# A dilated convolution by points on one core: matmuls issued in halves of the output rows, constants loaded on another queue, a second input's first points made later

## The chip, the cores and the metric

The kernel runs on one core of a Trainium2 chip. The metric is the device time of one execution in microseconds; less is better. PE is the matrix engine, DVE, ACT and POOL the vector, scalar and GpSimd engines, SP the engine that only issues transfers.

## What is computed

Input x is 4 images of 256 channels, 64x64, in float32. The part that the change touches is the first convolution and the weights that it uses:

```python
k = conv(x, w1, padding=6, rhs_dilation=2) + b1      # 256 -> 128 channels, 7x7
k = conv(k, w2) + b2                                 # 128 -> 49, 1x1
attn = softmax(k, axis=1)                            # 49 logits at every pixel
xp = pad(x, 6)
shifts = stack([xp[:, :, 2*u:2*u+64, 2*v:2*v+64] for u in range(7) for v in range(7)])
y = sum over the 49 taps of shifts * attn            # local attention
...
h = relu(bn(conv1x1(y, 256 -> 64)))
h = relu(bn(conv3x3(h, 64 -> 64)))
return relu(bn(conv1x1(h, 64 -> 256)) + y)
```

Batch norm uses the batch's own statistics. Everything from the softmax on lies after the changed stages.

## The kernel before

**The convolution by points.** w1 and w2 are composed into one 7x7 weight from 256 channels to 49 logits. Along the rows the convolution is evaluated at points: four pairs +p, -p and a last pass with the points 0 and infinity, so five passes n = 0 to 4. A pass needs its points (tile xi, x0 and x1 by strip), made on DVE from the row-sorted input (tile slots), and its weights, `weights(n, half)`. The 256 input channels are taken as two halves of 128 (`half` 0 and 1): all five passes are run for the first, then all five for the second.

**Strips.** The picture's columns are cut into four strips of eight. `column_convs(s, u, first)` (L247) does strip s, for x0 and x1 (i) and each of its eight columns (w): matmuls (L261) whose stationary operand is 128 columns of xi, and whose moving operand is 49 to 343 columns of weights. They add up in eight PSUM banks, acc[i][d], d = s-1, s, s+1. Two strips, half a picture, are 50 calls; a float32 matmul is two records in the profile, so 100 records.

**The first channel half.** Its passes after the first go in two half-pictures h, two strips each (loop at L466). `visit` makes the points of two strips (first `apply_factor` on the slots where the pass needs it; then `even`, `odd` and `mix`), `column_convs` uses them, and `put_aside` (L285, L286) copies finished banks to sv (three buffers) and stores them on ACT's queue in DRAM. DVE's and PE's order in this part is the order of the code (a manual schedule). Before it, `product` (L318) makes the weights of both channel halves by matmuls (L330) with w1 stationary, strided as loaded (w1raw) or copied (w1v); DVE and ACT write them out (L341 to L347).

**The second channel half is prepared meanwhile.** `fill_stage(h)` (L443) loads a half-picture of its 128 channels in 16 transfers on SP (L450, three raw buffers) and sorts them with 64 ACT copies (L169) into one tile, stage. `stage_parts(h)` (L453) makes pass 0's unmixed points x0 and x1 of the two strips, 12 DVE operations, and stores them (L459, SP); `stage_rows` (L462) stores the sorted rows, 4864 KB. Since there is one stage tile, `fill_stage(1)` comes behind `stage_parts(0)`. `load_ready` (L437) and `finish_parts` (two DVE operations per strip) bring the points back and mix them; `load_rows` (L430) brings the sorted rows into slots.

**The second channel half.** For each strip `put_back` (L612) loads what was put aside (L618 on SP, bks has four buffers), copies it on ACT into the PSUM banks (L619), and `column_convs` adds to it. `outputs` (L590; ACT copy L602, DVE L603, L604 and four more) turns two finished strips into logits. SP's order is by hand in pass 0; the rest is a scheduler's.

**Small loads.** Between the two channel halves, 16 small loads are issued on ACT's queue (L505 to L515): an identity, 1x1 weights, averaging and mask matrices, and batch norm parameters, in part of one element per partition. All are used behind the convolution.

`HALVES` is `(slice(0, 64), slice(64, 128))`. The local attention (L767), the 1x1 convolution (L800) and the moments (L1047) issue their matmuls in such halves already.

Of the kernel before, what the change touches and what calls it, by code (L numbers as in the profile page):

```python
# [48 lines left out]
P = 128  # L49
B, C, H, W = 4, 256, 64, 64  # L50
NH = C // P
K7 = 7
K = K7 * K7
PAD = 6
NT = H // 8
MID = 64
EPS = 1e-5
Q = 4
R = W // 2
# [9 lines left out]
NS, WS = 4, 8  # L69
# [7 lines left out]
CW = 16  # L77
# [17 lines left out]
def conv_seq_kernel(ctx: ExitStack, tc: tile.TileContext, xp, xt, w1, b1, w2t, b2, m1t, g1, be1,  # L95
# [154 lines left out]
    def column_convs(s, u, first):  # L250

        for d in (s - 1, s, s + 1):
            if not 0 <= d < NS:
                continue
            for i in range(2):
                for w in range(WS * s, WS * s + WS):
                    lo, hi = strip_taps(d, w)
                    if lo >= hi:
                        continue
                    o = (w - 3 + lo - WS * d) * K  # L260
                    nc.tensor.matmul(  # L261
                        acc[i][d][:, o : o + (hi - lo) * K],
                        xi[:, i, CW * w : CW * w + CW, :].rearrange("p x t -> p (x t)"),
                        u[i][:, lo * K : hi * K],
                        start=(first and w == max(0, WS * d - 3)),
                        stop=(w == min(R - 1, WS * d + WS + 2)),
                        skip_group_check=True,
                    )

    bks = pool(ctx, "bkp", 1).tile([P, 4, WS * K], F32, name="bks")  # L270
    n_back = [0]
# [2 lines left out]
    with ExitStack() as s1:  # L274
# [13 lines left out]
        with ExitStack() as s2:  # L288
# [29 lines left out]
            def product(w1raw, half, v, pw):  # L318

                wv = w1raw[:, :, v::K7].rearrange("p c u -> p u c")  # L320
                if half:
                    t = rawp.tile([P, 24, WP], F32, tag="raw", name="w1v").rearrange("p r w -> p (r w)")
                    t = t[:, : K7 * P].rearrange("p (u c) -> p u c", c=P)
                    nc.scalar.copy(t, wv)
                    wv = t
                for u in range(K7):

                    o = 0 if u == 0 else (2 + NP) * K if u % 2 else K
                    n = (1 + NP) * K if u in (0, K7 - 1) else NP * K
                    nc.tensor.matmul(  # L330
                        pw[:, o : o + n],
                        wv[:, u, :],
                        powers[:, u, :n],
                        start=(u == 0),
                        stop=(u == K7 - 1),
                        skip_group_check=True,
                    )
                c = slice((6 - v) * K, (7 - v) * K)
                ue = ut[:, half, 1 : 1 + NP, c]
                uo = pw[:, (2 + NP) * K : (2 + 2 * NP) * K].rearrange("p (i k) -> p i k", k=K)  # L340
                nc.scalar.copy(ue, pw[:, K : (1 + NP) * K].rearrange("p (i k) -> p i k", k=K))  # L341
                nc.scalar.copy(
                    ut[:, half, :: 1 + 2 * NP, c],
                    pw[:, : 2 * (1 + NP) * K].rearrange("p (a k) -> p a k", a=2)[:, :, :K],
                )
                nc.vector.tensor_tensor(ut[:, half, 1 + NP : 1 + 2 * NP, c], ue, uo, ALU.subtract)
                nc.vector.tensor_tensor(ue, ue, uo, ALU.add)  # L347
# [105 lines left out]
        def stage_parts(h, strips=range(2)):  # L453
            for s in strips:
                row = rows_of(stage, strip(s))
                for i, part in enumerate((even, odd)):
                    x = stgp.tile([P, SW, NT], F32, tag="x%d" % i, name="stage_x")
                    part(PAIRS[0], squares, row, x)
                    nc.sync.dma_start(out=ready[:, 2 * h + s, i], in_=x)  # L459
# [6 lines left out]
        for n, (p, factor, left) in enumerate(passes):  # L466
            if n == 0:
                continue
            u = weights(n, 0)
            for h in range(2):  # L470
                if factor is not None and (n, h) != (1, 0):
                    apply_factor(slots, factor, NR - 1 if n == 1 else NR - 2, strip(2 * h, 2))
                visit(slots, strip(2 * h, 2), p, left)
                if (n, h) == (2, 1):
                    stage_parts(0)
                    fill_stage(1)
                if (n, h) == (4, 0):
                    stage_parts(1, [0])
                    for s in range(2):
                        load_rows(s)  # L480
                if (n, h) == (4, 1):
                    stage_parts(1, [1])
                    load_ready(0)
                    finish_parts(0)
                    apply_factor(stage, squares[0], NR - 1)
                    stage_rows(1)
                    load_ready(1)
                    finish_parts(1)
                    for s in range(2):
                        apply_factor(slots, squares[0], NR - 1, strip(s))  # L490
                for s in range(2 * h, 2 * h + 2):
                    column_convs(s, u, True)
                    put_aside(n, s)
# [8 lines left out]
    pdiff_sb = late.tile([P, P], F32, name="pdiff_sb")  # L502
    bn12 = late.tile([P, 4], F32, name="bn12")
    bn3 = late.tile([P, 2, NH], F32, name="bn3")
    nc.scalar.dma_start(out=ident, in_=z)  # L505
    nc.scalar.dma_start(out=w1m, in_=m1t)
    nc.scalar.dma_start(out=pavg_sb, in_=pavg)
    nc.scalar.dma_start(out=pdiff_sb, in_=mask)
    for g in range(2):
        half = slice(g * MID, (g + 1) * MID)  # L510
        nc.scalar.dma_start(out=w3m[half, :], in_=m3t)
        for i, a in enumerate((g1, be1, g2, be2)):
            nc.scalar.dma_start(out=bn12[half, i : i + 1], in_=a[:, None])
    nc.scalar.dma_start(out=bn3[:, 0, :], in_=g3.rearrange("(n p) -> p n", p=P))
    nc.scalar.dma_start(out=bn3[:, 1, :], in_=be3.rearrange("(n p) -> p n", p=P))  # L515

    smp = pool(ctx, "smp", 2)
    outer = pool(ctx, "outerp", 1).tile([P, OUTER], F32, name="outer")

# [73 lines left out]
    def outputs(n, p, g):  # L593

        d = 2.0 * p * p
        for q in PAIRS:
            if q != p:
                d *= p * p - q * q
        m, t = (combs[:, 2 * i + n_combs[0] % 2] for i in range(2))
        n_combs[0] += 1  # L600
        a0, a1 = (accall[:, 4 * g + i : 4 * g + i + 3 : 2, : WS * K] for i in range(2))
        nc.scalar.copy(m, a0)  # L602
        nc.vector.tensor_tensor(t, a1, m, ALU.add)  # L603
        nc.vector.tensor_tensor(m, m, a1, ALU.subtract)  # L604
        for j in range(4):
            src, dst = (v.rearrange("p s v -> p (s v)") for v in (m if j % 2 else t, logit[:, g, j]))
            if n == 0:
                dst, src = (v.rearrange("p (w k) -> p w k", k=K) for v in (dst, src))
                stt(dst, src, p**j / d, bias_s)
            else:  # L610
                stt(dst, src, p**j / d, dst)
# [10 lines left out]
    with tc.manual_schedule(engines={mybir.EngineType.SP}):  # L622
        for s in range(2):
            put_back(0, s)
        for s in range(NS):
            if s in (1, 2):
                load_ready(s + 1)
                put_back(0, s + 1)
                load_rows(s + 1)
            if s > 1:  # L630
                finish_parts(s)
            column_convs(s, weights(0, 1), False)
            if s > 1:
                outputs(0, PAIRS[0], s - 2)
    for n, (p, factor, left) in enumerate(passes):
        if n == 0:
            continue
        u = weights(n, 1)
        if p is None:
            for s in range(NS):  # L640
                visit(slots, strip(s), p, left)
            for t in pads:
                nc.gpsimd.memset(t, 0.0)
        for s in range(NS):
            if n == 2 and s == NS - 1:
                apply_factor(slots, factor, NR - 2, strip(s))
            if p is not None:
                visit(slots, strip(s), p, left)
            if n == 1 and s:
                apply_factor(slots, passes[2][1], NR - 2, strip(s - 1))  # L650
            for d in ([s] if s == 0 else []) + ([s + 1] if s + 1 < NS else []):
                put_back(n, d)
            column_convs(s, u, False)
            if p is None:
                for d in range(s - 1 if s else 0, s + 1 if s == NS - 1 else s):
                    last_outputs(d)
            elif s > 1:
                outputs(n, p, s - 2)
            if p is None and 0 < s < NS - 1:
                if s == 2:  # L660
                    turn(0, 0)
                exponents(s - 1)
                shares(s - 1)
# [487 lines left out]
```

## Time and profile before

| | |
|---|---|
| median of three runs | 783.74 us (782.07 to 786.91) |
| the profiled execution | 784.71 us |
| its span | 782.9 us, 13023 instructions |
| mean granted clock of PE | 0.974 of full |
| matmuls of the convolution, L261 | 2000 records |
| points on DVE, L150 on the arena | 192 operations, 293.4 us |

The profile is of one execution. A group's line has the source line, engine, operation, what is written and read, the shape and the count; then busy time and the mean ns of one; then the engine's idle time ahead of them with what ended most of it. In the timeline, a line is a run of like operations: start, length, and in brackets the idle time before it and its releaser.

Where the 100 records of each half-picture of conv begin in the trace: 48.25 (pass 0, strips 0 and 1), 89.10, 107.84 (pass 1), 127.77, 149.92 (pass 2), 168.63, 188.20 (pass 3), 206.99, 225.71 (pass 4), 244.44; then the second channel half, passes 0 to 4, from 263.16, 308.29, 348.24, 387.48 and 424.94. The last ends near 466 us. All that follows, to 782.9, comes behind it.

### The profile page before, as it was taken

Reading aid. Unit: us, or ns where it says so; the run is one execution under the profiler, and the core shown is the slowest. Engines: PE = TensorE matmul, PEld = TensorE weight load, DVE = VectorE, ACT = ScalarE, POOL = GpSimd, SP = SyncE. Lnnn points to the kernel's source line nnn. Section 1 sums busy time; section 2 is a strip of 40 time slices with the busy share of each in tenths; the row PEclk is TensorE's granted clock in tenths of the full one; section 3 lists DMA queues with packets and bytes.
Section 4 is the critical chain, followed back from the end, with each engine's and each line's share of the span. In section 5 each row is a group of like instructions: output and inputs, shape, how many; then the busy total and the mean of one; then the engine's idle time right before and its main releaser. Section 6 shows DMA issues by size and latency. Waiting matters only on the chain.

```text
span 782.9 us, 13023 instructions
## 1 busy us (share of the span) xinstructions
PE 716.9 (92%) x5232; PEld 579.5 (74%) x5232; DVE 578.8 (74%) x685; ACT 304.7 (39%) x601; POOL 90.0 (12%) x155
## 2 busy tenths in 40 slices
PE   1969898999999979989999999999989988987995
PEld 1959787888888868868888888987878863436642
DVE  5899899999689769999999866322232248574797
ACT  4617465005611012110112139433444346346497
POOL 3416100000000020000002203322222200000000
PEclk9989999999999989999999999999999998998998
DMA  9741399626896984120111013476686759352298
GB/s 352 323 165 42 133 294 359 240 96 238 301 351 213 361 294 159 41 64 9 53 42 32 3 58 103 138 239 219 226 266 226 237 195 399 112 166 78 101 398 361
DMA packets 59823, 150.41 MB, mean 192 GB/s; under 512 B 7410, under 2 KB 35698, under 8 KB 56178
## 3 DMA queue, kind: packets, MB, share of 16 engines
q1 hardware_dynamic: 51792, 141.12, 50.5%
q10 hardware_dynamic: 7970, 8.45, 3.1%
q8 instruction: 41, 0.67, 0.3%
q14 instruction: 20, 0.16, 0.1%
HBM read 93.81 MB, written 55.74 MB: 191 GB/s over the span
## 4 chain that ended last, share of the span: by engine, by line
PE 59%; DVE 20%; DMA 9%; ACT 5%; issue 5%; POOL 1%; ACTq 1%; SPq 0%; DVEq 0%; POOLq 0%
PE acc L261 31%; DVE arena L150 13%; PE acc L767 9%; PE pconv L1029 4%; PE pconv L979 4%; DMA outer<-in_xt_dram 3%; PE acc L800 3%; PE pdirect L967 3%; DMA aside_dram<-sv 2%; PE acc L578 2%; DMA raw<-in_xp_dram 2%; DVE stage_x L150 2%; ACT arena L169 1%; PE pturn L1042 1%; ACT arena L585 1%
## 5 line engine op out<-in xcount | busy, mean ns | idle before, releaser
L261 PE MATMUL acc<-arena 128*128 128x196 f32 (+3 forms) x2000 | 385.3, 356 | 17.0 <-DVE arena L347 7.2
L261 PEld LDWEIGHTS acc<-arena 128*128 128x128 f32 x2000 | 324.9, 194 | 76.4 <-issue 13.1
L150 DVE SCALAR_TENSOR_TENSOR arena<-arena 128x1024 f32<-128x1024 f32 (+6 forms) x192 | 293.4, 1571 | 23.9 <-PE acc L261 17.3
L767 PEld LDWEIGHTS acc<-arena,outer 128*64 128x64 f32 x2048 | 112.7, 137 | 12.0 <-issue 11.4
L767 PE MATMUL acc<-arena,outer 128*64 128x128 f32 x2048 | 114.9, 273 | 6.7 <-issue 5.7
L808 DVE BATCH_NORM_STATS2 st<-acc 128x6 f32<-128x512 f32 x16 | 11.1, 695 | 66.3 <-PE acc L800 66.3
L122 ACT COPY outer<-outer 64x2048 f32<-64x2048 f32 x15 | 28.5, 1899 | 71.6 <-DMA outer<-in_xt_dram 71.6
L285 ACT COPY sv<-acc 128x392 f32<-128x392 f32 x40 | 19.2, 485 | 90.2 <-PE acc L261 66.3
L169 ACT COPY stage<-raw 128x128 f32<-128x128 f32 x128 | 43.9, 418 | 26.3 <-DMA raw<-in_xp_dram 25.1
L1029 PE MATMUL pconv<-arena,w3m 64*128 64x512 f32 (+1 forms) x144 | 42.8, 586 | 0.6 <-DVE arena L1086 0.6
L602 ACT COPY outer<-acc 128x784 f32<-128x784 f32 x8 | 6.5, 812 | 86.2 <-PE acc L261 86.2
L150 DVE SCALAR_TENSOR_TENSOR outer<-outer 128x784 f32<-128x784 f32 (+2 forms) x47 | 36.9, 840 | 3.6 <-ACT outer L921 3.6
L619 ACT COPY acc<-bks 128x392 f32<-128x392 f32 x40 | 18.4, 488 | 50.4 <-DVE outer L604 28.6
L1029 PEld LDWEIGHTS pconv<-arena,w3m 64*128 64x128 f32 x144 | 20.7, 185 | 21.9 <-DVE arena L1086 16.1
L123 POOL COPY outer<-outer 64x1792 f32<-64x1792 f32 x15 | 25.1, 1676 | 90.9 <-DMA outer<-in_xt_dram 90.9
L1091 ACT ACTIVATE outer<-arena 128x512 f32<-128x512 f32 (+1 forms) x58 | 34.7, 699 | 1.1 <-DVE arena L864 1.1
L1086 DVE SCALAR_TENSOR_TENSOR arena<-pconv,arena 128x512 f32<-128x512 f32 (+1 forms) x58 | 34.3, 674 | 0.0
L585 ACT COPY arena<-acc 128x512 f32<-128x512 f32 x52 | 27.1, 717 | 14.8 <-PE acc L578 14.8
L979 PE MATMUL pconv<-outer,arena 128*128 128x512 f32 x72 | 31.1, 592 | 0.0
L788 DVE COPY bks<-acc 128x256 f32<-128x256 f32 x32 | 11.3, 417 | 25.9 <-PE acc L767 25.9
L169 POOL COPY arena<-raw 128x192 f32<-128x192 f32 (+2 forms) x24 | 25.7, 1103 | 39.6 <-DVE arena L150 24.3
L800 PE MATMUL acc<-outer,w1m 128*64 128x512 f32 x64 | 28.8, 592 | 0.0
(147 smaller groups left out, 662.3 us busy)
## 6 DMA issues: line engine op xcount, KB each, us to landing
raw<-in_xp_dram SPq DMA_DIRECT2D x36, 608.0 KB, 5.6
outer<-in_xt_dram SPq DMA_DIRECT2D x17, 896.0 KB, 6.1
out_dram<-outer SPq DMA_DIRECT2D x14, 1024.0 KB, 4.7
arena<-y_dram SPq DMA_DIRECT2D x25, 512.0 KB, 8.4
fsort_dram<-stage SPq DMA_DIRECT2D x2, 4864.0 KB, 15.0
arena<-fsort_dram SPq DMA_DIRECT2D x8, 1216.0 KB, 8.7
y_dram<-outer SPq DMA_DIRECT2D x16, 512.0 KB, 4.7
aside_dram<-sv ACTq DMA_DIRECT2D x40, 196.0 KB, 5.7
```

Of the source, the lines that this page charges most:

```text
L122: nc.scalar.copy(t[:MID], x[MID:])
L123: nc.gpsimd.tensor_copy(t[MID:, : NT - 1], x[:MID, 1:])
L150: nc.vector.scalar_tensor_tensor(out, in0, scalar, in1, ALU.mult, ALU.add)
L169: (last if last and k + a == 2 else first if first and k + a == 0 else nc.scalar.copy)(d[:, k, :, PLACE[b], 2 * a : 2 * a + 2, i : i + count],
L261: nc.tensor.matmul(acc[i][d][:, o : o + (hi - lo) * K], xi[:, i, CW * w : CW * w + CW, :].rearrange("p x t -> p (x t)"), u[i][:, lo * K : ...
L585: nc.scalar.copy(dst, src)
L767: nc.tensor.matmul(dst[part, :: NT - 1] if edge else pts[c][part, o : o + 128], x[:, i, half * P + part.start : half * P + part.stop], ama ...
L800: nc.tensor.matmul(pt[a * MID : (a + 1) * MID, :], w1m[:, n, :], ys[a, n][:, 512 * i : 512 * i + 512], start=(n == 0), stop=(n == NH - 1), ...
L979: nc.tensor.matmul(m[k], wu[:, k, j, :], vs[k][:, g, j : j + R, :], start=(j == 0), stop=(j == 1))
L1029: nc.tensor.matmul(pt[:, :n], w3m[part, half * P : (half + 1) * P], h2[part, slot, q, lo : lo + n], start=True, stop=True)
L1086: nc.vector.scalar_tensor_tensor(v, conv3(b, q, i, half, lo, n), sc3[:, half : half + 1], v, ALU.mult, ALU.add)
L1091: nc.scalar.activation(dst, v.rearrange("p (r w) -> p r w", w=R), AF.Relu, bias=sh3[:, half : half + 1])
```

## The change

1. The matmul of `column_convs` and that of `product` are issued twice, once for each half of the output partitions (64 columns of the stationary operand each, the same moving operand).
2. The 16 small loads go from ACT's queue to SP's, and from between the channel halves to behind the strips of pass 0 of the second half. In SP's order they stand after `load_rows(3)` and before the put_back loads of passes 1 to 4.
3. `stage_parts(0)` and `fill_stage(1)` follow `visit` of pass 3, second half-picture, where they followed that of pass 2. `stage_parts(1)` follows whole the visit of (4, 1); before, its strips followed those of (4, 0) and (4, 1).

As built, two orders that the scheduler chooses differ as well: `finish_parts(3)` on DVE stands five visit operations later, behind the first `outputs` block and them, and the first points of pass 2 (strip 0) stand ahead of the ACT copy and the DVE additions of pass 1's last `outputs`, where they stood behind.

```diff
@@ column_convs
-                    nc.tensor.matmul(
-                        acc[i][d][:, o : o + (hi - lo) * K],
-                        xi[:, i, CW * w : CW * w + CW, :].rearrange("p x t -> p (x t)"),
...
+                    for part in HALVES:
+                        nc.tensor.matmul(
+                            acc[i][d][part, o : o + (hi - lo) * K],
+                            xi[:, i, CW * w : CW * w + CW, :].rearrange("p x t -> p (x t)")[:, part],
...
@@ product
-                    nc.tensor.matmul(
-                        pw[:, o : o + n],
-                        wv[:, u, :],
...
+                    for part in HALVES:
+                        nc.tensor.matmul(
+                            pw[part, o : o + n],
+                            wv[:, u, part],
...
@@ first channel half, behind visit(slots, strip(2 * h, 2), p, left)
-                if (n, h) == (2, 1):
+                if (n, h) == (3, 1):
                     stage_parts(0)
                     fill_stage(1)
                 if (n, h) == (4, 0):
-                    stage_parts(1, [0])
                     for s in range(2):
                         load_rows(s)
                 if (n, h) == (4, 1):
-                    stage_parts(1, [1])
+                    stage_parts(1)
                     load_ready(0)
                     finish_parts(0)
...
@@ before the second channel half
-    nc.scalar.dma_start(out=ident, in_=z)
-    nc.scalar.dma_start(out=w1m, in_=m1t)
...
@@ manual SP schedule of pass 0, behind its loop over strips
+        nc.sync.dma_start(out=ident, in_=z)
+        nc.sync.dma_start(out=w1m, in_=m1t)
+        nc.sync.dma_start(out=pavg_sb, in_=pavg)
+        nc.sync.dma_start(out=pdiff_sb, in_=mask)
+        for g in range(2):
+            half = slice(g * MID, (g + 1) * MID)
+            nc.sync.dma_start(out=w3m[half, :], in_=m3t)
+            for i, a in enumerate((g1, be1, g2, be2)):
+                nc.sync.dma_start(out=bn12[half, i : i + 1], in_=a[:, None])
+        nc.sync.dma_start(out=bn3[:, 0, :], in_=g3.rearrange("(n p) -> p n", p=P))
+        nc.sync.dma_start(out=bn3[:, 1, :], in_=be3.rearrange("(n p) -> p n", p=P))
```

More of the change, by code (lines that the diff above doesn't have):

```diff
@@ L260, in column_convs @@
                     o = (w - 3 + lo - WS * d) * K
-                    nc.tensor.matmul(
-                        acc[i][d][:, o : o + (hi - lo) * K],
-                        xi[:, i, CW * w : CW * w + CW, :].rearrange("p x t -> p (x t)"),
[L264 to L268, printed above, removed]
+                    for part in HALVES:
+                        nc.tensor.matmul(
+                            acc[i][d][part, o : o + (hi - lo) * K],
+                            xi[:, i, CW * w : CW * w + CW, :].rearrange("p x t -> p (x t)")[:, part],
+                            u[i][:, lo * K : hi * K],
+                            start=(first and w == max(0, WS * d - 3)),
+                            stop=(w == min(R - 1, WS * d + WS + 2)),
+                            skip_group_check=True,
+                        )
     bks = pool(ctx, "bkp", 1).tile([P, 4, WS * K], F32, name="bks")
@@ L329, in product @@
                     n = (1 + NP) * K if u in (0, K7 - 1) else NP * K
-                    nc.tensor.matmul(
-                        pw[:, o : o + n],
-                        wv[:, u, :],
[L333 to L337, printed above, removed]
+                    for part in HALVES:
+                        nc.tensor.matmul(
+                            pw[part, o : o + n],
+                            wv[:, u, part],
+                            powers[:, u, :n],
+                            start=(u == 0),
+                            stop=(u == K7 - 1),
+                            skip_group_check=True,
+                        )
                 c = slice((6 - v) * K, (7 - v) * K)
@@ L504, in conv_seq_kernel @@
     bn3 = late.tile([P, 2, NH], F32, name="bn3")
-    nc.scalar.dma_start(out=ident, in_=z)
-    nc.scalar.dma_start(out=w1m, in_=m1t)
[L507 to L515, printed above, removed]
     smp = pool(ctx, "smp", 2)
```

## The prediction, as put on record before the changed kernel ran

> **What bounds the kernel now.** I read the page's busy shares and chain of waits first, then the groups of instructions with shapes kept apart, then the timeline from 160 to 350 us, then busy time and clock by stretch.
>
> ```profile
> PE 716.9 (92%) x5232; PEld 579.5 (74%) x5232; DVE 578.8 (74%) x685; ACT 304.7 (39%) x601; POOL 90.0 (12%) x155
> PE acc L261 31%; DVE arena L150 13%; PE acc L767 9%; PE pconv L1029 4%; PE pconv L979 4%; DMA outer<-in_xt_dram 3%; PE acc L800 3%; PE pdirect L967 3%; DMA aside_dram<-sv 2%; PE acc L578 2%; DMA raw<-in_xp_dram 2%; DVE stage_x L150 2%; ACT arena L169 1%; PE pturn L1042 1%; ACT arena L585 1%
> ```
>
> PE is busy 92% of the span and the conv (L261) carries 31% of the chain, but DVE's points (L150) carry 13%: the two take turns. The timeline shows where.
>
> ```profile
> 181.18 18.31 DVE L150 SCALAR_TENSOR_TENSOR arena<-arena 128x2048 f32<-128x2048 f32 x8
> 206.50 9.25 DVE L150 SCALAR_TENSOR_TENSOR arena<-arena 128x2048 f32<-128x2048 f32 x4 [7.01 <-PE acc L261]
> 218.41 1.24 DVE L150 SCALAR_TENSOR_TENSOR stage_x<-stage 128x1024 f32<-128x1024 f32 x1 [2.67 <-ACT stage L169]
> ...
> 242.31 2.55 DVE L150 SCALAR_TENSOR_TENSOR arena<-arena 128x1024 f32<-128x1024 f32 x2
> 244.78 9.82 DVE L150 SCALAR_TENSOR_TENSOR stage<-stage 128x4608 f32<-128x4608 f32 x2
> ...
> 271.33 2.37 DVE L150 SCALAR_TENSOR_TENSOR arena<-arena 128x1024 f32<-128x1024 f32 x2 [4.39 <-PE acc L261]
> ...
> 286.73 1.23 DVE L150 SCALAR_TENSOR_TENSOR arena<-arena 128x1024 f32<-128x1024 f32 x1 [4.70 <-PE acc L261]
> 290.69 0.98 DVE L603 TENSOR_TENSOR outer<-acc,outer 128x784 f32<-128x784 f32 x1 [2.73 <-PE acc L261]
> ```
>
> The brackets are idle time and who ended it. From 92.6 to 199.5 us DVE has none; from 200 to 291 PE or the refilled stage holds it. The first strip of the second input half needs finish_parts (242.31), PE takes it only at 263.16, and DVE idles 4.39 + 0.22 + 4.70 + 2.73 = 12.0 us before 291. That is the reserve into which the stage's work can be moved. From 308.56 to 348.24 DVE idles 0.34 and sets the pace.
>
> ```profile
> 284.43 0.91 ACT L619 COPY acc<-bks 128x392 f32<-128x392 f32 x2 [14.25 <-issue]
> 284.98 60.91 PE L261 MATMUL acc<-arena 128*128 128x49 f32 x312 [4.33 <-ACT acc L619]
> ```
> ```profile
> 285.00:300.00 15.00, 15.00 (x72) 13.62 (x73) 10.54 (x11) 3.11 (x6) 0.00 (x0) 0.79 0.90 322
> 348.00:375.00 27.00, 26.76 (x134) 22.31 (x135) 26.28 (x24) 3.96 (x8) 0.00 (x0) 0.94 0.12 32
> ```
>
> ACT issues the 16 small loads, from 270.65 on, and the next put_back copy waits 14.25 us behind them; PE loses 4.33. In the windows (length, PE, PEld, DVE, ACT, POOL busy, granted clock, DMA share, GB/s) the clock then is 0.79: 15 x 0.21 = 3.2 us more.
>
> **Halves.** In the record of starts, conv matmuls of 343 to 147 columns follow each other at 288 to 125 ns, but 98 and 49 both at 112. Halves are in this trace already:
>
> ```profile
> L767 PE MATMUL acc<-arena,outer 128*64 128x128 f32 x2048 | 114.9, 273 | 6.7 <-issue 5.7 <-DMA outer<-in_xt_dram 0.8 <-POOL arena L729 0.2
> L1047 PE MATMUL moments<-outer 128*64 128x65 f32 x256 | 10.4, 232 | 0.9 <-DVE outer L1044 0.9
> ```
>
> 115 records of L767 start in the 6.3 us from 519.7: 54.8 ns each, 109.5 for two halves of 128 columns, what one full matmul of 128 would stream (between 125 for 147 and the 112 floor). Of L1047, 16 start in 0.46 us: 58 ns a pair of 65 columns. So two halves lie side by side and the floor goes: I take 57.5 ns for 49 (nearest row 58) and 84.5 for 98 (straight between 58 and 109.5). Half a picture's pass has 100 records, 12 of 49 and 12 of 98: 12 x 54.5 + 12 x 27.5 = 0.98 us of 18.73; bounds 0 (floor stays) and 12 x 54.5 + 12 x 54 = 1.3. Over 20 of them 19.6 us of PE time, but it counts only where PE is last. Doubled instructions alone cost nothing: L767 issues them at 54.8 ns, denser than any conv pair. The products' strided records (w1raw) come every 220 ns, where 196 columns of conv need 165 and 245 need 207: 70 x 55 + 28 x 13 = 4.2 us at most. But PE idles 7.2 us just ahead of 48.25 behind L347's DVE work; that stretch waits for DVE and the weights, so I take 0, and keep -4 to +1.
>
> The Trainium skill (TensorEngine Tiling (Array Packing), "Key Properties") says that changing the tiling mode drains TensorE: it speaks against mixing. Conv is alone on PE for nearly all its 385 us, and in halves throughout, and at the end the few transposes (L578) between conv strips would pay some; no row here isolates such a drain. Its "Instruction Overhead" section says a matmul has a fixed cost of about 60 cycles and that a dimension already small should not be split; by that the 49-column records would gain nothing, the 58 ns pair says otherwise.
>
> **Small loads.** Off ACT, the 14.25 us go to SP, behind load_rows(3) and ahead of 30 put_back loads, first needed for pass 1, 20 us later. 13.8 us of issuing there, by ACT's row; SP is otherwise idle for most of 275 to 308. I take 0; if the cover fails, pass 1's first copies wait up to 5 us. Gain: up to 4.33 + 3.2 = 7.5 us. But the next holder, the sv copy at 269.70, waited 9.49 us for an aside store queued behind the stage's 4864 KB store, so it stays, and the points of strip 2 come no earlier by this.
>
> **Moved stage work.** stage_parts is 12 DVE operations, 166.50 to 181.18: 14.7 us. It now follows visit (3,1). That visit overwrites points which PE reads in pass (2,1). With halves PE ends (2,1) at 184.4 (from the measured start of (1,1), 127.8 plus its DVE-limited 21, then 17.75 each), (4,1) at 255.4 instead of 263.16. visit (3,1): eight operations of 2.29 (18.31 / 8) make (3,0) and (3,1); of the last four (x0, x1, mix's two) x1's waits for PE at 184.4, so 184.4 + 3 x 2.29 = 191.3. stage_parts(0) to 206.0 (before 181.2). fill_stage(1) took the stretch from 181.26 to 218.41:
>
> ```profile
> 181.26:218.41 37.15, 36.45 (x196) 30.74 (x194) 27.27 (x13) 22.91 (x67) 0.60 (x1) 1.00 0.86 301
> ```
>
> DMA is at 0.86 and 301 GB/s: the transfers set its length, so I keep 37.2 us: 243.2. DVE makes (4,0) by 215.2 and (4,1) from 216.3, when PE leaves x0 of (3,1) (219.9 less the 3.6 us of its last x1 matmuls), to 225.5, and then idles 17.7 us. stage_parts(1) ends at 258.0, against 242.3: 15.7 late. The old reserve is 12.0, and it lay after this point, so at least 3.7 comes through if all of it can be used, 15.7 if none.
>
> Step by step: finish_parts(0) to 260.5 (PE free from 255.4: 5 us idle, and, as after the 4.33 gap, some 3 us of half clock). Stage factor 9.7, finish(1), two slot factors of 5: 283.8. Then three operations, outputs block 6.4, five visit operations that now stand before finish_parts(3), which ends at 304.7 (before about 300.8). PE strips of 8.3 to 9.4 us: strip 0 to 270, 1 to 282.7, 2 to 294, idle 8.4 until strip 3's points, to 315. Before, 308.3: so pass 0 of the second half ends 6 to 8 later, in spite of PE's own 7.8 head start. Pass 1 is DVE's: 39.7 us from 308.56 to 348.24, so pass 2 starts at 356 to 358, 8 to 10 late.
>
> What comes back: in passes 2 to 4 PE saves 6 x 0.98 = 5.9 us; DVE, next to be late, has only 27 - 26.28 plus 6.1 from 375 to 453 = 6.8 us idle there, so about all of it may. The half clock after the 2.36 us gap at 348.24 (0.94 over 27 us = 1.6 us) may go too, as that point now stands ahead of L592's block. Net 9 - 5.9 + 0 to 1.5 (new cold clock) = +3 to +6: I take +5. The tail from 466 is unchanged.
>
> **The rivals.** Faster: the refill goes at the page's best rate, 399 GB/s in place of 301: 37.15 x 301 / 399 = 28 us, so it ends at 234, stage_parts(1) at 248.8, 6.5 late and inside the reserve of 12. It decides below about 33 us. Then the end gains the 7.5 of the small loads and, of the 7.8 that halves save before 263, the half that DVE lets through, less 1 of new cold clock: -10.4, 774. For it: DMA at 0.86, not 1. Against: 301 is already high among the page's slices. 0.17.
>
> Slower: DVE keeps the 9 us. The late start of pass 2 isn't given back because the points stay last: DVE is 97% busy from 348 to 375, and waits for PE's release of points. It decides if less than 1.2 us of the 6.8 idle can be used: +9 and the strip-3 stall's 1.5 us of half clock: +10, 795. For it: the busy share; against: 22.73 of 25 us at 400. 0.27.
>
> Halves gain nothing on conv: the 112 ns floor is kept by 128 columns loaded in whatever pieces. Then +5 + 5.9 + 3.8 (pass (2,1) ends at 188.2 and all behind it moves) less 2 of slack: +13, 798. Against: 58 ns of L1047. 0.07. That halves lie one after the other would double 385 us of conv; L767 excludes it, 0.01.
>
> **How the numbers follow.** My sum goes against the profiled execution, 784.71 (span 782.9), which stands 1.0 above the median 783.74: 784.7 + 5 = 789.5; against the median, 788.7. I give 789. Forecast 0.48 (its own range 783 to 795). One per cent is 7.8 us, about what can be told from no change: below 776 faster, above 791.6 slower. Faster: the first rival 0.14 of its 0.17, forecast 0.02. Slower: second rival 0.22, third 0.07, forecast's tail 0.10. The range, 775 to 799, leaves out 0.10 of the first rival and some 0.08 of the second's and third's upper ends.
>
> **What would show it.** Right: 4000 records of conv, pairs of 49 every 57 ns; stage_parts(1)'s first operation at 243 after an idle of 17 on ACT stage L169; no 14.25 at L619; PE waiting for DVE at strip 3 near 302; pass 2's start at 356. Wrong: stage_parts(1) before 235 (first rival), pass 3's end 8 or more late (second), pairs at 112 (third).

## The result, and the profile after

The changed kernel takes 796.38 us (median of six runs, 790.45 to 797.64), the kernel before 783.27 (six runs). The ratio is 1.0167, 95% interval 1.0136 to 1.0198: slower by 13.1 us, where +5 was forecast. The profiled execution took 795.75 us, its span is 793.9.

The page's busy shares and the chain of waits by line, after (line numbers are those of each kernel's own file, so conv's L261 is L262 here and put_back's copy, L619, is L608; they shift again in the runs below):

```profile
PE 705.9 (89%) x7428; PEld 520.8 (66%) x7428; DVE 579.6 (73%) x685; ACT 305.8 (39%) x601; POOL 90.8 (11%) x155
PE acc L262 19%; DVE arena L150 18%; PE acc L767 13%; DMA raw<-in_xp_dram 6%; DVE arena L1086 4%; PE acc L800 4%; PE pconv L979 3%; DVE stage_x L150 3%; PE pdirect L967 3%; PE acc L567 2%; DVE outer L150 2%; DMA ready_dram<-stage_x 1%; PE pturn L1042 1%; ACT arena L574 1%; PE moments L1047 1%
```

PE is busy 11 us less, and DVE hardly more (579.6 against 578.8). Yet conv's share of the chain fell from 31% to 19%: its place was taken by DVE's points (13 to 18%), by the loads of the stage's refill (2 to 6%) and by a line that was not in the chain's list, a store of stage_x. (The local attention, L767, rose from 9 to 13%, where loads of its own, 3% before, left the list.) So the time is not work added, it is waiting. DVE's timeline shows where (start, length, count, and in brackets the wait and who ended it):

```profile
241.94 1.26 DVE L150 SCALAR_TENSOR_TENSOR stage_x<-stage 128x1024 f32<-128x1024 f32 x1 [14.62 <-ACT stage L169]
...
257.75 1.23 DVE L150 SCALAR_TENSOR_TENSOR stage_x<-stage 128x1024 f32<-128x1024 f32 x1 [8.14 <-DMA ready_dram<-stage_x]
...
265.07 2.55 DVE L150 SCALAR_TENSOR_TENSOR arena<-arena 128x1024 f32<-128x1024 f32 x2
...
360.04 0.97 DVE L592 TENSOR_TENSOR outer<-acc,outer 128x784 f32<-128x784 f32 x1 [2.86 <-PE acc L262]
```

The first line is the forecast one: stage_parts(1) starts at 241.94 (forecast 243.2) after an idle of 14.6. The second was not forecast at all. The second strip writes the same two stage_x buffers as the first, so it waits for the first strip's store, 8.14 us. Before, the points of a whole half-picture stood between the two strips, and there was no wait:

```profile
223.42 2.55 DVE L150 SCALAR_TENSOR_TENSOR stage_x<-stage,stage_x 128x1024 f32<-128x1024 f32 x2
225.89 9.15 DVE L150 SCALAR_TENSOR_TENSOR arena<-arena 128x2048 f32<-128x2048 f32 x4
234.97 1.22 DVE L150 SCALAR_TENSOR_TENSOR stage_x<-stage 128x1024 f32<-128x1024 f32 x1
```

After, finish_parts(0) comes at 265.07 (forecast 258.0, before 242.31), and from there to 357 DVE has no idle to take it up. PE's timeline, for the same stretch:

```profile
266.39 11.38 PE L262 MATMUL acc<-arena 128*64 128x196 f32 x88 [9.34 <-DVE arena L150]
...
303.03 7.58 PE L262 MATMUL acc<-arena 128*64 128x196 f32 x68 [5.57 <-DVE arena L150]
```

PE, done with the first channel half at 257.1, waits 9.34 us for points. The first strip then takes 11.38 us, at a granted clock of 0.75; in a run below (the transfers in order), after a wait of 1.69, it takes 8.56 at 1.00. Why the store was late is in the transfers that SP issued, and in the windows (length, PE, PEld, DVE, ACT, POOL busy, granted clock, DMA share, GB/s) of the same 29 us, after (first) and before (second):

```profile
237.02 2.29 SPq L432 DMA_DIRECT2D arena<-fsort_dram  x4
245.83 4.13 SPq L461 DMA_DIRECT2D ready_dram<-stage_x  x2
```
```profile
237.00:266.00 29.00, 20.05 (x236) 13.79 (x232) 15.49 (x13) 9.24 (x24) 0.00 (x0) 0.93 1.00 382
```
```profile
237.00:266.00 29.00, 29.00 (x151) 24.32 (x150) 28.69 (x15) 3.82 (x9) 0.00 (x0) 1.00 0.72 281
```

Four loads of 1216 KB (load_rows) are issued as soon as the refill's last loads are, the store stands behind them, and lands 11.9 us after its issue; before, no such store took over 3.9. The DMA engines are busy all 29 us at 382 GB/s, where before they were at 0.72. What had been spread over the stretch from 181 to 260 is now asked for at once, on the path.

### The profile page after: what moved, and what is told of

It reads as the page before. It is cut to its first block, busy times and chain, and to the rows that moved or that the text cites. A ratio compares the mean times of both kernels' runs of the same rounds, so it can differ in the third digit from the quotient of the medians.

```text
span 793.9 us, 17411 instructions
## 1 busy us (share of the span) xinstructions
PE 705.9 (89%) x7428; PEld 520.8 (66%) x7428; DVE 579.6 (73%) x685; ACT 305.8 (39%) x601; POOL 90.8 (11%) x155
## 4 chain that ended last, share of the span: by engine, by line
PE 47%; DVE 33%; DMA 8%; issue 5%; ACT 5%; POOL 1%; SPq 0%; ACTq 0%; DVEq 0%; POOLq 0%
PE acc L262 19%; DVE arena L150 18%; PE acc L767 13%; DMA raw<-in_xp_dram 6%; DVE arena L1086 4%; PE acc L800 4%; PE pconv L979 3%; DVE stage_x L150 3%; PE pdirect L967 3%; PE acc L567 2%; DVE outer L150 2%; DMA ready_dram<-stage_x 1%; PE pturn L1042 1%; ACT arena L574 1%; PE moments L1047 1%
## 5 line engine op out<-in xcount | busy, mean ns | idle before, releaser
L262 PE MATMUL acc<-arena 128*64 128x294 f32 (+6 forms) x4000 | 374.9, 349 | 36.4 <-DVE arena L150 26.0
L262 PEld LDWEIGHTS acc<-arena 128*64 128x64 f32 x4000 | 270.8, 140 | 139.6 <-issue 38.6
L150 DVE SCALAR_TENSOR_TENSOR arena<-arena 128x1024 f32<-128x1024 f32 (+7 forms) x192 | 295.1, 1586 | 13.9 <-PE acc L262 7.9
L767 PE MATMUL acc<-arena,outer 128*64 128x128 f32 x2048 | 115.3, 273 | 10.1 <-issue 7.0
L767 PEld LDWEIGHTS acc<-arena,outer 128*64 128x64 f32 x2048 | 112.7, 137 | 15.6 <-issue 13.4
L608 ACT COPY acc<-bks 128x392 f32<-128x392 f32 x40 | 18.7, 488 | 57.0 <-DVE outer L593 34.9
L788 DVE COPY bks<-acc 128x256 f32<-128x256 f32 x32 | 11.3, 417 | 25.5 <-PE acc L767 25.5
L169 ACT COPY arena<-raw 128x192 f32<-128x192 f32 (+2 forms) x36 | 20.5, 647 | 22.0 <-DVE arena L150 15.0
```

The costliest lines, as they stand in the source:

```text
L150: nc.vector.scalar_tensor_tensor(out, in0, scalar, in1, ALU.mult, ALU.add)
L169: (last if last and k + a == 2 else first if first and k + a == 0 else nc.scalar.copy)(d[:, k, :, PLACE[b], 2 * a : 2 * a + 2, i : i + count],
L262: nc.tensor.matmul(acc[i][d][part, o : o + (hi - lo) * K], xi[:, i, CW * w : CW * w + CW, :].rearrange("p x t -> p (x t)")[:, part], u[i][ ...
L767: nc.tensor.matmul(dst[part, :: NT - 1] if edge else pts[c][part, o : o + 128], x[:, i, half * P + part.start : half * P + part.stop], ama ...
```

## The experiments

Each ratio is against the kernel before in runs on the same chip.

**The three parts, each alone, and two together.** The edits are the hunks of the change, so they are not shown again.

> Only the matmuls of conv and of the weights in halves. Theory A (the moved stage work costs the time): halves save 0.98 us per half-picture wherever PE is last, nine times before the second channel half and part of it after: -5 to -9 us, near 776; conv's half-pictures are 17.75 us apart. Theory B (the halves themselves cost, through twice the instructions: 1 to 1.8 us gaps named issue in the local attention, 3.7 us more there in the changed kernel): conv ends 4 to 6 us earlier but the local attention gives it back: 780 to 786. Theory C (the small loads on SP cost): as A.

> Only the 16 small loads on SP's queue. Theory A: PE's wait of 4.33 us at the first strips goes, but strip 2's points come no earlier, and DVE has the next wait: 0 to -4 us. Theory B: as A. Theory C (16 issues of some 18 us on SP ahead of the put_back loads of pass 1): pass 1 waits for its copies, +3 to +8 us.

> Only the stage work made later. Theory A: stage_parts(1)'s second strip waits some 8 us for its store, the second channel half starts 10 or more later, DVE has no idle until pass 2: +13 to +19 us, 797 to 802, more than the whole change. Theory B: +5 to +9. Theory C: +5 to +8.

> Halves and small loads, the stage work where it was. Theory A: -6 to -11 us, 772 to 777, faster than either alone. Theory B: 780 to 784. Theory C: 0 to +3 against halves alone plus 3 to 8.

| kernel | median, us | ratio, 95% interval |
|---|---|---|
| halves alone | 782.66 | 0.9989 [0.9952, 1.0027] |
| small loads alone | 782.04 | 0.9987 [0.9950, 1.0024] |
| moved stage work alone | 798.44 | 1.0195 [1.0121, 1.0269] |
| halves and small loads | 778.22 | 0.9958 [0.9922, 0.9994] |

The moved stage work is the whole loss (theory A): alone it costs 15 us, as much as the change or more. The other two bring little alone and 3 us together, by the ratio: less than A expected of halves (5 to 9) and of the two (6 to 11). By its number, 782.66, halves alone lies in B's range. But B's reason isn't there: conv is not followed by a longer local attention in this run (144.7 us, 144.3 before; more under Scatter). Where the gain goes is in PE's timeline of halves alone:

```profile
189.83 89.61 PE L262 MATMUL acc<-arena 128*64 128x196 f32 x976 [4.40 <-DVE arena L150]
285.26 49.49 PE L262 MATMUL acc<-arena 128*64 128x49 f32 x554 [5.82 <-ACT acc L621]
```

PE is faster and waits: 4.40 us for the points of pass 3 (0.69 and 2.41 in two profiles of before), 5.82 for the put_back copy behind the small loads (4.33 and 1.71 before), and 2.47 at 337 (2.36 before, at 348). With the small loads off ACT the second wait goes. That the two parts together bring more than the sum of each alone is not clear of the noise.

**The store's wait taken away.** Three edits of the changed kernel, and one with halves and moved stage work only. The first gives the second strip of stage_parts(1) its own buffers:

```diff
-                    x = stgp.tile([P, SW, NT], F32, tag="x%d" % i, name="stage_x")
+                    if h and s:
+                        x = rawp.tile([P, ROWS2, WP], F32, tag="raw", name="raw").rearrange("p r w -> p (r w)")
+                        x = x[:, : SW * NT].rearrange("p (x t) -> p x t", t=NT)
+                    else:
+                        x = stgp.tile([P, SW, NT], F32, tag="x%d" % i, name="stage_x")
```

> The changed kernel, with stage_parts(1)'s second strip written to two of the raw buffers, which are idle by then, so that it does not wait for the first strip's store. Theory A1 (the store's wait of 8.14 us is paid in full, as DVE has no idle until pass 2): stage_parts(1) runs 14.8 us without a break, and 6 to 8 us come off: 788 to 790. Theory A2 (the lateness of the refill alone sets it, and the wait is hidden by what follows): 0 to -2, 794 to 797.

793.97 us, ratio 1.0129 [1.0075, 1.0182], against the changed kernel's 1.0167 no difference that is clear of the noise. The wait went from its place and came back eight microseconds later, in DVE's timeline:

```profile
246.18 1.22 DVE L150 SCALAR_TENSOR_TENSOR stage_x<-stage 128x1024 f32<-128x1024 f32 x1
247.44 2.67 DVE L150 SCALAR_TENSOR_TENSOR stage_x<-stage,stage_x 128x1024 f32<-128x1024 f32 x2
...
265.95 2.55 DVE L150 SCALAR_TENSOR_TENSOR arena<-arena 128x1024 f32<-128x1024 f32 x2 [8.03 <-DMA arena<-ready_dram]
```

stage_parts(1) now runs through, and finish_parts(0) waits 8.03 us for load_ready(0), which SP issues only at 258, behind the stores and in the same traffic. A1 fell in its number, and A2 had not named this reason. The second edit asks for load_rows later:

```diff
                 if (n, h) == (4, 0):
-                    for s in range(2):
-                        load_rows(s)
...
                     stage_parts(1)
+                    for s in range(2):
+                        load_rows(s)
```

> The changed kernel, with load_rows(0) and (1) asked for behind stage_parts(1) in place of behind visit (4, 0). Theory A1 with the cause that the store landed 11.9 us after its issue because four loads of 1216 KB were issued just before it: the store lands in 3 to 5 us, the wait falls from 8.14 to 0 to 2, and the time by 4 to 8, to 788 to 792. If the store is late for another reason (the stage's fill, ACT's stores), the wait stays and the time is 795 to 798.

798.71 us, 1.0180 [1.0117, 1.0243]: no gain. The store's waits shrink to 1.48 and 1.62 with two or three of the four loads ahead of it in place of all four, so the loads had been the main reason; but SP's order, which the scheduler makes, put the others between the stores and ahead of load_ready, and the wait moved once more:

```profile
252.98 1.25 DVE L150 SCALAR_TENSOR_TENSOR stage_x<-stage 128x1024 f32<-128x1024 f32 x1 [1.48 <-DMA ready_dram<-stage_x]
...
269.08 2.55 DVE L150 SCALAR_TENSOR_TENSOR arena<-arena 128x1024 f32<-128x1024 f32 x2 [6.93 <-DMA arena<-ready_dram]
```

The third moves the stage work half as far:

```diff
-                if (n, h) == (3, 1):
+                if (n, h) == (3, 0):
                     stage_parts(0)
                     fill_stage(1)
```

> The changed kernel, with stage_parts(0) and fill_stage(1) one half-picture earlier, behind visit (3, 0): about 15 us earlier than in the changed kernel, some 10 later than before. Theory A: the refill ends near 228, stage_parts(1) still stands whole behind visit (4, 1), which it now waits for only by DVE's order: the second channel half starts 9 to 14 us earlier than in the changed kernel: 780 to 786. If not lateness but the place of stage_parts(1) in one piece costs: 790 to 796.

778.12 us, 0.9918 [0.9886, 0.9950], 18 us below the changed kernel (by the ratios 19 to 20) and a little faster than before. A wait of the same length stands in DVE's timeline:

```profile
242.31 1.24 DVE L150 SCALAR_TENSOR_TENSOR stage_x<-stage 128x1024 f32<-128x1024 f32 x1 [8.12 <-DMA ready_dram<-stage_x]
```

but finish_parts(0) is then done at 252.3, with PE still in the first channel half (it begins the second at 255.8). So the wait costs nothing 15 us earlier: stage_parts(1) in one piece is no loss, and finish_parts(0) may be 7.5 us later than before (249.8 against 242.31) at no cost. What goes beyond PE's end is paid.

> Halves and the moved stage work, small loads on ACT as before. Theory A: DVE sets the pace from the late stage work to pass 2, so halves bring only what passes 2 to 4 give, and the small loads' ACT time falls into a wait for DVE: 0 to -4 us against the moved stage work alone, 794 to 798, as the whole change. If halves bring their full 5 to 6 us: 791 to 793.

801.12 us, 1.0200 [1.0141, 1.0259], above both ranges: halves gave nothing against the moved stage work alone (1.0195). In this run the refill ends at 243.97 and finish_parts(0) is at 267.6: who waits for transfers is not helped by a faster PE.

**The transfers in order, with the stage work as late.** Order on SP by hand, in the changed kernel with the raw buffers of the first edit:

```diff
-                if (n, h) == (4, 0):
-                    for s in range(2):
-                        load_rows(s)
                 if (n, h) == (4, 1):
-                    stage_parts(1)
-                    load_ready(0)
-                    finish_parts(0)
...
+                    with tc.manual_schedule(engines={mybir.EngineType.SP}):
+                        for s in range(2):
+                            load_ready(s)
+                        stage_parts(1)
+                        for s in range(2):
+                            load_rows(s)
+                        finish_parts(0)
...
```

> The changed kernel with the transfers between the refill and the first strip put in order on SP: load_ready(0) and (1) first, the four stores of stage_parts(1) (second strip from idle raw buffers), and only then load_rows(0) and (1). The stage work stays as late as in the changed kernel. Theory D (waits that took each other's place, 8.14 us on a store, 8.03 and 6.93 us on load_ready in the two experiments before, are one cause: some 10 MB asked for at once from 237 us on): stage_parts(1) ends at 257 and finish_parts(0) follows without a wait: 6 to 8 us off the changed kernel, 788 to 790. Theory E (lateness of the refill alone, the transfers only fill a wait that is there anyway): 794 to 797.

785.92 us, 1.0039 [1.0004, 1.0073]: 10.5 us below the changed kernel (10.0 by the ratios), so more than theory D asked. The buffers alone, the first edit, had brought about 3, not clear of the noise. DVE's timeline from the stage's refill on:

```profile
241.93 1.41 DVE L150 SCALAR_TENSOR_TENSOR stage_x<-stage 128x1024 f32<-128x1024 f32 x1 [12.13 <-ACT stage L169]
...
254.87 2.52 DVE L150 SCALAR_TENSOR_TENSOR raw<-stage,raw 128x1024 f32<-128x1024 f32 x2
257.31 2.54 DVE L150 SCALAR_TENSOR_TENSOR arena<-arena 128x1024 f32<-128x1024 f32 x2
```

The refill ends when it did (241.93 against 241.94); finish_parts(0) comes at 257.31 in place of 265.07, with no wait between, and PE idles 1.69 us there in place of 9.34. The window from 237 to 266 has DMA at 0.84, not 1.00. Behind this block the scheduler ordered DVE's operations somewhat differently (the first outputs block stands later), so that a part of the 10.5, perhaps the 2 us above the wait's 8, may come from that.

> The same order of transfers, with stage_parts(0) and fill_stage(1) behind visit (3, 0), as in the run that was half as far. Theory D: its 8.12 us wait for the store goes, DVE reaches the second channel half before PE does, and PE has next to no idle there: 768 to 774. Theory E: 776 to 779, as without the order.

776.50 us, 0.9915 [0.9884, 0.9947], the same as half as far without the order: theory E's number, for the reason seen above, that the wait was covered there.

**What was left.** PE still waits for a put_back copy, 8.55 us at 290 in the run with the transfers in order. The next edit puts load_rows(2) and (3) on SP behind the put_back loads of strips 2 and 3:

```diff
             if s in (1, 2):
                 load_ready(s + 1)
                 put_back(0, s + 1)
-                load_rows(s + 1)
+            if s == 2:
+                load_rows(2)
+                load_rows(3)
```

> The run with transfers in order and the late stage work, and on SP load_rows(2) and (3) behind put_back of strips 2 and 3, so that these no longer stand behind a load that waits for the stage's 4864 KB store. Theory D2 (the rest of the loss, some 3 us over before, is that order: PE waited 8.55 us on the copy of strip 3's put_back at 290): that wait goes, 4 to 8 us come off, 778 to 782, and nothing of the changed kernel's loss is left. Theory E2 (the rest is the lateness itself, DVE is the next holder): 784 to 787.

> The same with the stage work half as far: PE's waits of 6.90 and 3.66 us on put_back copies go, 770 to 774 by theory D2; 775 to 778 if DVE or the put_back loads behind the small loads hold it.

784.88 us, 1.0020 [0.9990, 1.0051], and 775.30, 0.9891 [0.9868, 0.9914]: about 1 us each, inside the noise, not the 4 to 8 expected. The wait stayed, in PE's timeline of the first:

```profile
289.27 2.34 PE L262 MATMUL acc<-arena 128*64 128x49 f32 x24 [8.22 <-ACT acc L612]
```

The edit had moved the wrong loads. The 24 records that wait are the last of strip 1: they come behind strip 0's 88 and strip 1's first 88, and they add to strip 2's banks. So they wait for the put_back of strip 2, and its loads stood ahead of load_rows(2) already without this edit, as SP's timeline of the run with the transfers in order shows:

```profile
269.73 0.32 SPq L468 DMA_DIRECT2D fsort_dram<-stage  x1
270.16 1.45 SPq L439 DMA_DIRECT2D arena<-ready_dram  x2
271.70 2.41 SPq L611 DMA_DIRECT2D bks<-aside_dram  x2
286.57 0.80 SPq L432 DMA_DIRECT2D arena<-fsort_dram  x2
```

What stands ahead of them is the stage's 4864 KB store. In the edited run that was issued at 269.47 and landed at 285.8, and the slowest put_back load took 16.5 us to land, where the median is 3.1. So D2 was not put to the test: no run here issues these loads ahead of the store. In the second run the same wait was 7.07 us, and PE also waited 3.90 us at 306 for put_back copies, whose loads stand behind the small loads on SP. 775.30 is the lowest time found here, though not clear of 776.50: all three parts, the stage work half as far, transfers in order.

**Scatter.** Two more profiles were taken, of the kernel before and of halves alone.

> The kernel before once more, for a second profile of it: how far the end of conv (466.0 us) and the local attention's stretch (144.3 us from its first to its last matmul) vary from one execution to another. If halves lengthen the local attention: 143 to 145 here. If it is scatter: up to 148.

> The halves alone once more, for a second profile: end of conv 460.4 in the first, local attention as before. If halves lengthen the local attention: 147 to 151 us. If it is scatter: between 144 and 151.

| profile | end of conv, us | local attention, first to last matmul, us |
|---|---|---|
| before, first and second | 466.0, 461.1 | 144.3, 150.7 |
| halves alone, first and second | 460.4, 462.9 | 144.7, 146.0 |
| changed kernel | 473.7 | 148.0 |

The 3.7 us that the local attention took longer in the changed kernel is inside what the kernel before does from one execution to another, so no run here puts it down to a part of the change. The second profile of before has its wait behind the small loads at 1.71 us instead of 4.33, and conv ends 4.9 us earlier. The forecast's sum stood against the first.

## Why the forecast was wrong, step by step

**Halves: right in the stage, too large in the end.** The forecast had 17.75 us between half-pictures; the trace has 17.75 (150.36 to 168.11 and on). That the saving of 0.98 us came out to the digit is in part luck. "98 and 49 both at 112" misread the record of starts: in pass 3, from 387 us, the two records of one matmul of 49 columns start 42 or 71 ns apart, and the next matmul follows 110 to 112 later. The mean time from the start of a record to the next, before (387 to 443 us), and from pair of halves to pair, after (397 to 450), is:

| columns | before, ns | after, ns | saved |
|---|---|---|---|
| 49 | 82 | 50 | 32 |
| 98 | 116 | 89 | 27 |
| 147 | 141 | 127 | 14 |
| 196 | 172 | 168 | 4 |

The forecast had 54.5 and 27.5 for the first two and nothing below. 49 columns saved less, 147 and 196 saved where it had nothing, and the sum, 0.94 us over 12, 12, 12 and 16 records, is nearly the same. The Trainium skill (TensorEngine Tiling (Array Packing), "Instruction Overhead") advises against splitting a dimension that is small already. The prediction read this as saying that 49 columns would gain nothing; but what is split here is the 128 columns of the other operand, and 82 ns became 50. Its "Key Properties" warn of a drain at a change of mode. Among conv's last strips, PE's next conv record starts 1.00 to 1.02 us after the first of eight transposes (L567), and 0.87 to 0.88 before the change: 0.14 us more, in which a drain may have its part, 0.6 in all four such places. But halves alone made no measurable difference: PE was not last for long enough, as the waits of 4.40 and 5.82 us showed.

**Small loads: little, as the sum had it.** "Up to 7.5 us" became 1 us, with the interval on both sides of zero. PE's wait of 4.33 us went; in its place PE waits 4.44 us for DVE's points at 335.6 (before, 2.36 at 348). The cost on SP that was taken as 0 is not seen in the changed kernel; in the fastest version it may be in the 3.90 us above.

**Moved stage work: right to the refill, wrong behind it.** Measured against forecast: visit (3, 1) ended at 193.0 (191.3), stage_parts(0) at 207.9 (206.0), the refill at 241.9 (243.2). The step that failed is "stage_parts(1) ends at 258.0", and the "finish_parts(0) to 260.5" built on it. They were costed at DVE's own 14.8 us, as if no transfer stood in it. The waits that the sum lacked are 8.14 us for a store out of two buffers used twice and, where that is taken away, 8.03 for the load_ready behind it; in the kernel before, a visit of 9.2 us lay between the two strips and covered the store. Instead of 258.0 and 260.5 the trace has 265.07 and 267.6, 7 us more. Most of that delay went on: finish_parts(3) ended at 310.9 (304.7).

The rest of the account is not a plain sum. Pass 2 began at 359.55 (356 to 358), so a part was made good on the way. Passes 2 to 4 gave back 3.7 us, not the 5.9 that halves were to save there: 117.8 us from pass 2's start to conv's end before, 114.1 after. So conv ends 7.7 us later than in the profile that the sum stood against, where its own terms give 3.1 to 4.6 (9 - 5.9 + 0 to 1.5; +5 is rounded up), and 12.6 later than in the second profile of before. That +5 and the missing 7 come near the measured +13.1 is therefore no proof; the experiments carry the cause. The run with the transfers in order takes the missing wait out and comes out at +3 [0.3, 5.7], about the forecast, though 10 us and not 7 came off.

**The scheduler's order.** PE had 5.57 us, not 8.4, of idle behind strip 2, as pass 1's strip 0 was put ahead of pass 0's strip 3 on PE; that order was not in the sum.

**The rivals.** The slower one named the sign and nearly the size (795), but not the mechanism: it had DVE keep 9 us in the passes behind. In fact more was lost earlier, and some of it was given back: pass 2 began 11.3 us late, pass 3 9.7 and pass 4 7.7. The faster one needed a refill under 33 us; it took about 34 from 207.9. It also held that a delay inside the reserve would be free, and the run half as far showed just that, with finish_parts(0) 7.5 us late. That halves gain nothing on conv's rounds was wrong: 17.75 us.

What stays open: how much of the 10.5 us is the transfers' order and how much the scheduler's new order on DVE behind them. And of the +3 left, whether it is the lateness or the put_back load behind the stage's store; the run meant to tell moved other loads and left that wait in its place.

## What to carry to other kernels

When a step is moved later, cost its transfers in the new place too: what had been spread over 80 us may be asked for in 30, and a store that never took over 3.9 us takes 11.9. Where one buffer is used twice, look for what lay between the two uses: it was the cover. And when a wait is taken away and the time stays, look for the same number one step further on: the wait was a sign of the cause, not the cause. Before moving a transfer out of the way of another, count which records wait, and check that the one moved stands ahead of the one they wait for.

## What was not expected of the hardware

Two halves of 49 columns pass in 50 ns together, against a mean of 82 for one full-width record, and below the 58 ns that the moments' pair of 65 columns had shown. Their two streams run side by side: in pass 3 the second half's record starts 2 to 10 ns after the first's. And with the DMA engines at a share of 1.00 and 382 GB/s, a 512 KB store's time to landing went from a median of 3.4 us to 11.9.
